# Attention hybrid of four images: turns of token blocks taken from TensorE and given to VectorE and DMA, one diagonal block handled as the others, a scratch tensor loaded in pieces

## The chip, the cores and the metric

The kernel runs on one core of one Trainium2 chip, in float32. The metric is the time of one execution on the device in microseconds (us), taken as the median of several runs. Traces come from one profiled execution.

## What is computed

The input is four images `x` of 128 channels by 64 x 64 points (4096 tokens of 128 numbers each). The reference, cut to what matters here:

```python
x = x + conv_attention(group_norm(x))       # layer 0: softmax(q k^T) v, a gate, a projection
t = to_tokens(x)                            # (4 images, 4096 tokens, 128)
def attn(u):                                # layer 1, u = layer norm of t
    q = u @ W
    return softmax(q @ q.T) @ u
t = t + attn(ln(t))
t = t + recurrence(batch_norm(ln(t) @ Wf.T))   # y_t = sigmoid(wx_t + y_{t-1} V^T) over the tokens
```

Layer 1's score matrix `q q^T` is symmetric. The kernel uses that: it computes a block of exponentials once and uses its transpose for the mirrored block.

## The kernel before

**Tiling.** Each image has 4096 tokens, cut into 8 blocks of 512 (`NB` = 8), each of 4 groups of 128 (`NQ` = 4). For each of the four images the kernel runs layer 0 (`layer0`, with `attention`, L220) and then layer 1 (`layer1`, L560). A scan over the recurrence (L971 on) ends the program.

**Layer 1.** The rows run in the order n = 6, 7, 5, 4, 3, 2, 1, 0. A row takes its blocks a = n, n-1, ..., 0, each in two steps (i = 0, 1). A step computes scores (L810, TensorE), exponentials (L816, ScalarE), and, two steps later, the product with the tokens of block a (`direct`, L681). For a < n the exponentials are also turned: VectorE transposes 32 x 32 blocks within `dd` (L651), and 16 DMAs carry the pieces to their partitions in `tt` (`send`, L661: 12 issued by SyncE, SP, and 4 by ScalarE, ACT). Four steps later TensorE multiplies the turned tile (`reversed_products`, L694), which adds to row a. There are two `dd` buffers and three `tt` buffers.

**Diagonal blocks.** For a = n > 1 (`upper`) only the upper triangle of the 4 x 4 groups is computed (score widths 512, 384, 256, 128), the six groups above the diagonal are turned in the same way, and `own_products` (L671, three products of widths 384, 256, 128) adds the lower triangle, three steps after the block. For the blocks n = 1 and n = 0, `quarter` (L585) computes the full first half and lets TensorE transpose four 128 x 128 groups (L596).

**End of a row block.** When all parts of block n are summed in `oacc` (`part`, L701), `finish` (L712) puts three functions in a queue. `tokens` (L733) lets TensorE transpose the four groups of `oacc` (L736), takes the denominators (L741), adds the residual `t` and normalises (`layernorm`, L298, with one power on GpSimd, POOL). `turn` (L755) lets TensorE transpose the four groups of the normalised tokens (L758), ScalarE copies them out of PSUM (L759), and `result` sends `t` off by `turn_out`. `inputs` (L765) multiplies by the recurrence's weights (L767) and stores the product in `wxs_d`.

**A move.** Layer 0 already turns its blocks of 128 x 512 without TensorE (`move`, L289): `turn_out` (L275) transposes 32 x 32 blocks on VectorE (L280), issues four DMAs on SP (L284) that write a DRAM scratch `turn_d` with the blocks in their turned places, and one more DMA on SP (L294) reads the scratch back to the destination.

**What sets the order.** Deferred functions wait in the deque `pending`; work of the next image (`prepare`: norms, projections, gates, put up at L941) waits in `ahead`. A step of layer 1 runs one function of `pending`, else one of `ahead` (L842); an empty function `nothing` stands as a delay and gives its turn to `ahead`. Layer 0 takes `ahead` first. `flush` (L215) runs what must be complete before a row. A scheduler then orders the instructions of each engine by its own estimates, except in a few parts written as fixed. TensorE, VectorE, ScalarE and SP each execute their instructions in that order.

**The last image.** At the start of its layer 1, three DMAs of 2 MB (L947) load the recurrence's inputs of images 0 to 2 from `wxs_d` into `wxs`, which takes the buffer of layer 0's operands.

Of the kernel before, what the change touches and what calls it, by code (L numbers as in the profile page):

```python
# [10 lines left out]
F32 = mybir.dt.float32  # L11
I32 = mybir.dt.int32
AF = mybir.ActivationFunctionType
ALU = mybir.AluOpType
# [4 lines left out]
P = 128  # L19
# [150 lines left out]
        )  # L170


def fast(
    tc, x, out, t_d, t2_d, wxs_d, turn_d, wt, col, par, par2, bpc, bc, ident, gavg, quart,
    own, shift, inv_sqrt, par_ok, load, scales, shifts, written,
# [15 lines left out]
    with ExitStack() as st:  # L191
# [10 lines left out]


        ahead: deque = deque()
        pending: deque = deque()

        def nothing():

# [6 lines left out]
        def flush(until=None):  # L215

            while pending and until not in done:
                pending.popleft()()

        def attention(score_mm, bias, scale, weigh, finish, need):  # L220


            fifo: deque = deque()
            o = None
            left = len(pending)

            def pop():
                nonlocal o
                n, p, e, acc = fifo.popleft()
                if p == 0:  # L230
                    o = None
                o = weigh(o, n, p, e)
                if p == PAIRS - 1:
                    finish(n, o, acc)

            for n in range(NB):
                acc = first = None
                for p in range(PAIRS):
                    need(n, p)
                    ps = ps_s.tile([P, 2, QB], F32, tag="s", name="ps")  # L240
                    for h in range(2):
                        lhsT, rhs = score_mm(n, p, h)
                        nc.tensor.matmul(ps[:, h, :], lhsT=lhsT, rhs=rhs, start=True, stop=True)  # L243
                    e = ep.tile([P, 2, QB], F32, tag="e", name="e")
                    nc.scalar.activation(e, ps, AF.Exp, scale=scale)  # L245
                    if p == 0:
                        first = e
                    elif p == 1:
                        acc = accp.tile([P, 2, QB], F32, tag="acc", name="acc", bufs=2)
                        nc.vector.tensor_tensor(acc, first, e, ALU.add)  # L250
                    else:
                        nc.vector.tensor_tensor(acc, acc, e, ALU.add)  # L252
                    fifo.append((n, p, e, acc))
                    if len(fifo) > LAG:
                        pop()
                        if p == 0:
                            pop()
                    if ahead:
                        ahead.popleft()()
                    elif pending and (p % 2 == 0 or left > 0 or len(pending) > 6):  # L260
                        left -= 1
                        pending.popleft()()
            while fifo:
                pop()

# [204 lines left out]
        def layer0(b, gate, q, k, v, need):  # L470
# [20 lines left out]
            def finish(n, o, acc):  # L491
# [60 lines left out]
                    nc.gpsimd.tensor_scalar(hn, hn, 1.0, None, ALU.add)  # L552
                    done.add((b, n))

                pending.extend([sums, nothing, denominators, projection, nothing, tokens])

            attention(score_mm, None, SCALE, weigh, finish, need)
            return h, qt
# [1 line left out]
        def layer1(b, h, qt):  # L560
# [6 lines left out]
            tt = big.tile([P, 3, NQ * QB], F32, tag="tt", name="tt")  # L567
            fifo: deque = deque()
            own_turned: deque = deque()

            unsent: deque = deque()
            turned: deque = deque()
# [40 lines left out]

            def upper(n, a):

                return a == n > 1

# [45 lines left out]
            def own_products():  # L665

                _, n, t, o = own_turned.popleft()
                assert fifo and fifo[-1][0] == n
                t = t[:, : 4 * 6 * 32].rearrange("q (p s k) -> q p s k", p=4, s=6)
                for j, s in ((3, 3), (2, 1), (1, 0)):  # L670
                    nc.tensor.matmul(  # L671
                        o[:, : j * P], lhsT=h[:, NQ * n + j, :],
                        rhs=t[:, :, s : s + j, :].rearrange("q p k j -> q k p j"),
                        start=False, stop=False,
                    )
# [25 lines left out]
            def part(n, o):  # L701
# [7 lines left out]
                if parts[n] == NB - n - (b == B - 1 and n == 0):  # L709
                    finish(n)  # L710

            def finish(n):  # L712
                cs = bass.ts(n, QB)
                rinv = stat.tile([P, NQ], F32, tag="rinv", name="rinv")
                t = work.tile([P, 4, NQ, 32], F32, tag="t", name="t1", bufs=2)
                if b == B - 1 and n == 0:
# [5 lines left out]
                    def bank():  # L722
                        return ps_o.tile([P, QB], F32, tag="o", name="ml")
# [9 lines left out]
                def tokens():  # L733
                    m = bank().rearrange("q (j c) -> q j c", j=NQ)
                    for j in range(NQ):
                        nc.tensor.transpose(m[:, j, :], oacc[:, n, bass.ts(j, P)], ident)  # L736
                    if b == B - 1 and n == 0:
                        take_banks()
                    at = (B + b) * NT + n * NQ
                    den = den_all[:, at : at + NQ]  # L740
                    nc.vector.tensor_reduce(den, m, AX.X, ALU.add)  # L741
                    nc.vector.tensor_scalar(den, den, 1.0 / C, None, ALU.mult)
                    nc.vector.reciprocal(rinv, den)
                    for j in range(NQ):
                        nc.vector.scalar_tensor_tensor(
                            t1[:, j, :].rearrange("q (p i) -> q p i", p=4),
                            m[:, j, :].rearrange("q (p i) -> q p i", p=4), rinv[:, j : j + 1],
                            t[:, :, j, :], ALU.mult, ALU.add,
                        )
                    layernorm(quarters(t1), quarters(h2))  # L750
# [12 lines left out]
                    result()  # L763

                def inputs():  # L765
                    m = bank()
                    nc.tensor.matmul(m, lhsT=wt["f"], rhs=th, start=True, stop=True)  # L767
                    nc.vector.bn_stats(bn_st[:, b * NB + n, :], m)
                    m = m.rearrange("p (g i s) -> p i g s", i=L // 2, s=2)
                    if b == B - 1 and n == 0:  # L770
                        last_inputs.append(m)
                    elif b == B - 1:
                        nc.vector.tensor_copy(wxs[:, :, b, bass.ts(n, GB), :], m)
                    else:
                        wx = work.tile([P, L // 2, GB, 2], F32, tag="wx", name="wx")
                        nc.vector.tensor_copy(wx, m)
                        nc.sync.dma_start(wxs_d[b, :, :, bass.ts(n, GB), :], wx)

                if b == B - 1 and n == 0:
                    pending.appendleft(tokens)  # L780
                    pending.extend([turn, inputs])
                elif b == B - 1 and n == 1:
                    pending.extend([tokens, nothing, turn, inputs])
                elif b == B - 1 and n < 4:
                    pending.extend([tokens, turn, inputs])
                else:
                    pending.extend([tokens, nothing, nothing, nothing, turn, inputs])


            for n in [NB - 2, NB - 1] + list(range(NB - 3, -1, -1)):  # L790
# [4 lines left out]
                for a in order(n):  # L795
# [4 lines left out]
                    for i in range(2):  # L800
                        ps = ps_s.tile([P, 2, QB], F32, tag="s", name="ps")
                        e = ep.tile([P, 2, QB], F32, tag="e", name="e")
                        if a == n < 2 and i == 1:
                            quarter(n, ps, e, before)
                        else:
                            width = 0
# [24 lines left out]
                            queries(NB - 1)  # L831
                        fifo.append((n, a, i, e, o))
                        clock += 1
                        if len(fifo) > LAG:
                            direct()
                            if a == order(n)[0] and i == 0:
                                direct()
                        if own_turned and own_turned[0][0] <= clock:
                            own_products()
                        if turned and turned[0][0] <= clock:  # L840
                            reversed_products()
                        if pending:  # L842
                            pending.popleft()()
                        elif ahead:
                            ahead.popleft()()
                    if turns(n, a) or upper(n, a):
                        send(n, a, d, t, nc.sync, range(3))
                        unsent.append(partial(send, n, a, d, t, nc.scalar, (3,)))
                    if upper(n, a):
                        own_turned.append((clock + 3, n, t, o))  # L850
                    elif turns(n, a):
# [5 lines left out]
            if b == B - 1:  # L857

                ordered.enter_context(tc.manual_schedule())
            pending.extend([reversed_products] * len(turned))  # L860

# [71 lines left out]
        for b in range(B):  # L935
# [3 lines left out]
            if b < B - 1:  # L939
                parts0, norm, chunks, gates = prepare(b + 1, own_bank)  # L940
                ahead.extend(norm + sum(chunks, []) + gates)  # L941
            else:


                wxs = keep.tile([P, L // 2, B, G, 2], F32, tag="next", name="wxs")
                for i in range(B - 1):
                    nc.sync.dma_start(wxs[:, :, i, :, :], wxs_d[i])  # L947
            layer1(b, h, qt)
            while ahead:
                ahead.popleft()()  # L950
# [491 lines left out]
```

## Time and profile before

| what | value |
|---|---|
| median of 3 runs | 3017.7 us (3017.13 to 3018.09) |
| profiled execution | 3015.99 us, its span 3014.3 us |
| mean granted TensorE clock | 0.995 |
| TensorE (PE) busy | 2961.1 us of the span |
| VectorE (DVE), ScalarE (ACT), GpSimd (POOL) busy | 1716.2, 1016.1, 223.1 us |
| layer 0 of image 1 (777 to 1101 us) | 324 us, PE busy 324.00 |
| layer 1 of image 1 (1101 to 1500 us) | 399 us, PE busy 396.83, DVE 200.10, ACT 111.17 |
| layer 1 of image 3 (2544 to 2932 us) | 388 us, PE busy 381.08 |

A row of the profile's timeline gives the start, the time from the first start to the last end, the engine, the line, the operation, the tiles written and read, and the count; brackets hold the engine's idle time before it and what ended it. A float32 matmul appears as two records, a transpose on TensorE as one. "SPq" and "ACTq" are the DMA issues of SP and ACT; they do not count as busy time.

### The profile page before, as it was taken

The page shows a single profiled execution, that of the slowest core. Times are in us where ns is not written, and L with a number is a line of the kernel's source. Part 1 is how long each engine was busy: PE and PEld are TensorE (multiplying, and loading weights), DVE is VectorE, ACT ScalarE, POOL GpSimd, SP SyncE. Part 2 cuts the span into 40 slices and gives each one's busy share as a digit, 9 for nine tenths or more (in the row PEclk, how much of TensorE's full clock was granted, in tenths as well). Part 3 has the DMA queues.
Part 4 walks back from the last instruction along what each step waited for, and adds up shares of the span by engine and source line. Part 5 has one row for each costly group of instructions (what it writes and reads, how often), then busy time and mean ns, then how long its engine had stood idle before and what let it go on. Part 6 is the DMA issues. An engine that isn't in the chain of part 4 may idle for free.

```text
span 3014.3 us, 32549 instructions
## 1 busy us (share of the span) xinstructions
PE 2961.1 (98%) x10774; PEld 1378.9 (46%) x10774; DVE 1716.2 (57%) x3208; ACT 1016.1 (34%) x1123; POOL 223.1 (7%) x216
## 2 busy tenths in 40 slices
PE   8999999999999999999999999999999999999995
PEld 4444444444444444444444444444444444444443
DVE  6666654544666664544466666554556666344456
ACT  4444422222344432222244443222234444222224
POOL 0111100000011110000011101000001111000000
PEclk9999999999999999999999999999999999999998
DMA  1112144434122134444312114444422113544434
GB/s 42 41 54 57 50 130 105 100 95 111 31 56 57 43 90 112 102 104 106 74 46 56 42 47 127 104 106 99 106 46 56 41 48 91 147 108 104 111 94 186
DMA packets 265425, 250.62 MB, mean 83 GB/s; under 512 B 96160, under 2 KB 180640, under 8 KB 264224
## 3 DMA queue, kind: packets, MB, share of 16 engines
q1 hardware_dynamic: 239328, 216.95, 27.2%
q10 hardware_dynamic: 25920, 31.49, 4.2%
q8 instruction: 89, 1.46, 0.2%
q14 instruction: 88, 0.72, 0.1%
HBM read 65.80 MB, written 56.62 MB: 41 GB/s over the span
## 4 chain that ended last, share of the span: by engine, by line
PE 94%; DVE 2%; DMA 1%; ACT 1%; SPq 0%; issue 0%; ACTq 0%; POOL 0%; DVEq 0%
PE o L485 29%; PE o L681 15%; PE ps L243 15%; PE ps L810 14%; PE ot L694 13%; PE o L671 1%; PE m L272 1%; PE m L767 1%; PE mp L378 1%; PE mp L447 1%; DMA wxs<-wxs_d 1%; PE mp L432 1%; DVE t2s L1020 1%; DVE ps_r L991 1%; PE mq L582 1%; PE m L736 1%
## 5 line engine op out<-in xcount | busy, mean ns | idle before, releaser
L485 PE MATMUL o<-e,nxt 64*128 64x512 f32 x4096 | 966.4, 589 | 0.0
L245 ACT ACTIVATE e<-ps 128x1024 f32<-128x1024 f32 x512 | 521.6, 1025 | 687.6 <-PE ps L243 656.1
L252 DVE TENSOR_TENSOR acc<-acc,e 128x1024 f32<-128x1024 f32 x448 | 547.3, 1222 | 231.7 <-ACT e L245 216.0
L485 PEld LDWEIGHTS o<-e,nxt 64*128 64x128 f32 x4096 | 400.1, 187 | 483.0 <-issue 474.2
L816 ACT ACTIVATE e<-ps,shift 128x1024 f32<-128x1024 f32 (+2 forms) x282 | 298.7, 1060 | 729.2 <-PE ps L810 431.2
L243 PE MATMUL ps<-nxt 64*128 64x512 f32 x2048 | 533.1, 595 | 1.2 <-ACT e L245 0.6
L681 PE MATMUL o<-e,h 128*128 128x512 f32 (+3 forms) x1160 | 511.4, 567 | 0.0
L810 PE MATMUL ps<-qt 128*128 128x512 f32 (+3 forms) x1128 | 501.9, 567 | 4.0 <-ACT qt L583 2.7
L651 DVE STREAM_TRANSPOSE dd<-e 128x512 f32<-128x512 f32 x444 | 287.3, 687 | 306.2 <-ACT e L816 217.5
L694 PE MATMUL ot<-tt,h 128*128 128x512 f32 x888 | 402.2, 593 | 0.0
L681 PEld LDWEIGHTS o<-e,h 128*128 128x128 f32 x1160 | 220.2, 191 | 259.0 <-issue 248.3
L810 PEld LDWEIGHTS ps<-qt 128*128 128x128 f32 x1128 | 208.1, 190 | 230.0 <-issue 208.1
L243 PEld LDWEIGHTS ps<-nxt 64*128 64x128 f32 x2048 | 194.9, 187 | 229.6 <-issue 148.7
L694 PEld LDWEIGHTS ot<-tt,h 128*128 128x128 f32 x888 | 164.2, 190 | 186.9 <-issue 185.5
L145 POOL TENSOR_SCALAR rstd<-mv 128x4 f32<-128x4 f32 x64 | 14.6, 228 | 2349.7 <-DVE mv L309 2349.7
L703 DVE TENSOR_TENSOR oacc<-oacc,ot 128x512 f32<-128x512 f32 x87 | 59.3, 682 | 162.2 <-PE ot L694 162.2
L541 DVE SCALAR_TENSOR_TENSOR t<-yt,rinv,t 128x128 f32<-128x128 f32 x128 | 36.5, 347 | 79.6 <-DMA yt<-turn_d 79.6
L502 POOL TENSOR_SCALAR xb<-xb,bpc 128x512 f32<-128x512 f32 x32 | 63.4, 1981 | 245.1 <-DMA xb<-in_x_dram 230.5
L552 POOL TENSOR_SCALAR h<-h 128x512 f32<-128x512 f32 x32 | 72.4, 2262 | 63.8 <-DVE d L280 63.8
L146 POOL TENSOR_TENSOR rstd<-rstd,mhalf 128x4 f32<-128x4 f32 x64 | 66.4, 1038 | 5.3
L390 ACT ACTIVATE nxt<-mp,par 64x512 f32<-64x512 f32 x31 | 23.9, 772 | 114.7 <-DVE nxt L386 101.2
L312 DVE TENSOR_SCALAR h<-t,mv,rstd 128x128 f32<-128x128 f32 x128 | 35.7, 343 | 46.9 <-POOL rstd L146 46.9
(165 smaller groups left out, 1578.4 us busy)
## 6 DMA issues: line engine op xcount, KB each, us to landing
tt<-dd SPq DMA_DIRECT2D x1332, 64.0 KB, 2.0
tt<-dd ACTq DMA_DIRECT2D x444, 64.0 KB, 2.0
turn_d<-d SPq DMA_DIRECT2D x384, 64.0 KB, 1.8
nxt<-in_x_dram SPq DMA_DIRECT2D x16, 512.0 KB, 5.5
xb<-in_x_dram SPq DMA_DIRECT2D x32, 256.0 KB, 3.3
t<-turn_d SPq DMA_DIRECT2D x32, 256.0 KB, 2.7
yt<-turn_d SPq DMA_DIRECT2D x32, 256.0 KB, 2.6
t_d<-t SPq DMA_DIRECT2D x32, 256.0 KB, 2.0
```

What stands on the lines that cost most here:

```text
L146: nc.gpsimd.tensor_tensor(dst, dst, mhalf[:, :n], ALU.pow)
L243: nc.tensor.matmul(ps[:, h, :], lhsT=lhsT, rhs=rhs, start=True, stop=True)
L245: nc.scalar.activation(e, ps, AF.Exp, scale=scale)
L252: nc.vector.tensor_tensor(acc, acc, e, ALU.add)
L485: nc.tensor.matmul(o[r], lhsT=v[rs, p + h * PAIRS, :], rhs=e[rs, h, :], start=(p == 0 and h == 0), stop=(p == PAIRS - 1 and h == 1),)
L502: biased = nc.gpsimd.tensor_scalar(xb, xb, bpc, None, ALU.add)
L552: nc.gpsimd.tensor_scalar(hn, hn, 1.0, None, ALU.add)
L651: nc.vector.transpose(d.rearrange("q f b k j -> q k b f j")[:, 2 * i + half], e[:, half, :].rearrange("q (b f j) -> q b f j", b=NQ, f=NQ),)
L681: nc.tensor.matmul(o[:, cols], lhsT=h[:, NQ * a + 2 * i + half, :], rhs=es, start=(a == order(n)[0] and i == 0 and half == 0), stop=(a == ...
L694: nc.tensor.matmul(ot, lhsT=h[:, NQ * n + j, :], rhs=t.rearrange("q (p b k j) -> q b k p j", p=4, b=NQ, k=NQ)[:, j], start=(j == 0), stop= ...
L810: nc.tensor.matmul(scores, lhsT=qt[:, bass.ts(at, P)], rhs=qt[:, n * QB + cols.start : n * QB + cols.stop], start=True, stop=True,)
L816: nc.scalar.activation(e.rearrange("p a b -> p (a b)")[:, :width], ps.rearrange("p a b -> p (a b)")[:, :width], AF.Exp, bias=shift,)
```

## The change

Seven edits:

1. `finish_moved` replaces `finish` for all eight blocks of images 0 to 2 and for blocks 4 to 7 of image 3. Both transposes on TensorE become moves: `oacc` is moved in `sums`, the normalised tokens in `tokens`. The copy out of PSUM by ACT is gone. Blocks 0 to 3 of image 3 keep the old way.
2. `pending` becomes a `Work` object: chains of (delay, function) in which a later chain may run beside an earlier one as long as it stays two functions behind. Its clock advances by 2 in a step of layer 1 and by 1 in a step of layer 0.
3. The diagonal block n = 1 is now `upper`; `quarter` serves n = 0 alone.
4. `own_products` stands ahead of the step's `direct` products.
5. Of a turned tile with a < n, SP issues 8 DMAs and ACT 8. Diagonal tiles keep 12 and 4.
6. The load of `wxs` is cut into 12 DMAs of 0.5 MB, taken one at a time through `ahead`.
7. In layer 0, the deferred functions get the delays 0, 4, 2, 4.

```diff
+    def may(self, c):
+        b = c["before"]
+        if c["ready"] > self.now:
+            return False
+        if b is None or not b["tasks"]:
+            return True
+        return c["behind"] is not None and b["count"] > c["count"] + c["behind"]
...
-                pending.extend([sums, nothing, denominators, projection, nothing, tokens])
+                pending.add([(0, sums), (4, denominators), (2, projection), (4, tokens)], behind=None)
...
             def upper(n, a):
-                return a == n > 1
+                return a == n > 0
...
+            def finish_moved(n):
+                cs = bass.ts(n, QB)
+                rinv = stat.tile([P, NQ], F32, tag="rinv", name="rinv")
+                t = ot = th = None
+                def sums():
+                    nonlocal t, ot
+                    t = work.tile([P, 4, NQ, 32], F32, tag="t", name="t1", bufs=2)
+                    nc.sync.dma_start(t, t_d[b, n])
+                    ot = work.tile([P, 4, NQ, 32], F32, tag="og", name="otk")
+                    move(oacc[:, n, :].rearrange("c (j f k) -> c j f k", j=NQ, f=4), flat(ot))
+                def tokens():
+                    nonlocal th
+                    reciprocals(n, ot.rearrange("q p j i -> q j p i"), AX.XY, rinv)
+                    for j in range(NQ):
+                        nc.vector.scalar_tensor_tensor(
+                            t[:, :, j, :], ot[:, :, j, :], rinv[:, j : j + 1], t[:, :, j, :],
+                            ALU.mult, ALU.add,
+                        )
+                    h2 = work.tile([P, 4, NQ, 32], F32, tag="h2", name="h2m")
+                    layernorm(tiles(t), tiles(h2))
+                    th = work.tile([P, QB], F32, tag="th", name="thm")
+                    move(h2.rearrange("q p j i -> q j p i"), th)
+                    turn_out(t.rearrange("q p j i -> q j p i"), t2_d[b, :, cs])
+                def inputs():
+                    recurrence_inputs(n, th, ps_m.tile([P, QB], F32, tag="m", name="mw"))
+                pending.add([(0, sums), (8, tokens), (8, inputs)])
...
             def finish(n):
+                if b < B - 1 or n >= 4:
+                    return finish_moved(n)
...
                 elif b == B - 1 and n < 4:
-                    pending.extend([tokens, turn, inputs])
+                    pending.add([(0, tokens), (2, turn), (2, inputs)])
...
-                        if a == n < 2 and i == 1:
+                        if a == n == 0 and i == 1:
                             quarter(n, ps, e, before)
...
+                        if own_turned and own_turned[0][0] <= clock:
+                            own_products()
                         if len(fifo) > LAG:
                             direct()
                             if a == order(n)[0] and i == 0:
                                 direct()
-                        if own_turned and own_turned[0][0] <= clock:
-                            own_products()
...
-                        if pending:
-                            pending.popleft()()
-                        elif ahead:
-                            ahead.popleft()()
+                        if not pending.run():
+                            nothing()
+                        pending.now += 2
                     if turns(n, a) or upper(n, a):
-                        send(n, a, d, t, nc.sync, range(3))
-                        unsent.append(partial(send, n, a, d, t, nc.scalar, (3,)))
+                        own = 3 if upper(n, a) else 2
+                        send(n, a, d, t, nc.sync, range(own))
+                        for f in range(own, NQ):
+                            unsent.append(partial(send, n, a, d, t, nc.scalar, (f,)))
...
-                for i in range(B - 1):
-                    nc.sync.dma_start(wxs[:, :, i, :, :], wxs_d[i])
+                pieces = [
+                    (wxs[:, bass.ts(r, L // 8), i, :, :], wxs_d[i, :, bass.ts(r, L // 8)])
+                    for i in range(B - 1) for r in range(4)
+                ]
+                ahead.extend(partial(nc.sync.dma_start, *piece) for piece in pieces)
```

`reciprocals` and `recurrence_inputs` hold the former lines 739 to 743 and 767 to 777 unchanged.

## The prediction

> **What bounds the kernel now.** I read the page's first and fourth parts, then the waits of PE, the timeline around the edited lines, and the chain in order of time.
>
> ```profile
> PE 2961.1 (98%) x10774; PEld 1378.9 (46%) x10774; DVE 1716.2 (57%) x3208; ACT 1016.1 (34%) x1123; POOL 223.1 (7%) x216
> ...
> PE 94%; DVE 2%; DMA 1%; ACT 1%; SPq 0%; issue 0%; ACTq 0%; POOL 0%; DVEq 0%
> ```
>
> PE is busy for 98% of the span and carries 94% of the chain. So a matmul taken off PE is worth its issue time, and a matmul that waits costs its wait. What PE waits for in layer 1 is one line:
>
> ```profile
> PE o L671 <- DMA tt<-dd: 3.8, 2, 2.7
> ```
>
> Those are the first diagonal blocks (n = 6) of images 1 and 3. The timeline shows how tight they are, and what an issue costs:
>
> ```profile
> 1427.75 0.60 PE L736 MATMUL m<-ident,oacc 128*128 128x128 f32 x4
> ...
> 1428.11 2.53 ACTq L661 DMA_DIRECT2D tt<-dd  x4
> ...
> 1428.19 2.74 PE L694 MATMUL ot<-tt,h 128*128 128x512 f32 x6
> ...
> 1437.99 1.00 SPq L284 DMA_DIRECT2D t_d<-d  x2
> ...
> 1443.22 1.46 PE L671 MATMUL o<-tt,h 128*128 128x384 f32 x6
> ...
> 1444.52 0.60 PE L758 MATMUL m<-ident,h 128*128 128x128 f32 x4
> ```
>
> Four transposes occupy PE for 1428.19 - 1427.75 = 0.44 us. A send costs ACT 2.53/4 = 0.63 us of issue, a write of a move costs SP 0.50 us.
>
> ```profile
> 2551.70 9.08 DMA wxs<-wxs_d
> 2560.80 13.84 DMA wxs<-wxs_d
> ```
>
> ```profile
> 2580.47 2.05 PE L671 MATMUL o<-tt,h 128*128 128x384 f32 x3 [2.65 <-DMA tt<-dd]
> ```
>
> ```profile
> 2580.00:2610.00 30.00, 29.53 (x65) 13.74 (x66) 12.14 (x30) 5.57 (x5) 2.76 (x3) 0.89 0.50 128
> ```
>
> In image 3 the three loads of `wxs` sit ahead of the diagonal's sends and PE waits 2.65 us. The last row, a window of busy times, has the granted clock as the third number from its end: 0.89. The clock records put a half-rate stretch of 6.8 us there.
>
> **The change, part by part.**
>
> *Turns off PE.* 28 blocks lose 8 transposes each. The start-to-start times of all 248 such records of the 31 ordinary blocks sum to 29.4 us, 0.95 us a block (the rows above give 0.88). 28 x 0.95 = **-26.6 us**. All of it is on the path.
>
> [...] a move is a VectorE transpose of 0.69 us, four issues (2.0), a landing (1.8, the page's median), a read-back (2.7), some 7.2 us against 0.44 us. If those 7.2 us, twice a block, stood on the path, the sum would be 28 x 14.4 = 403 us worse. They don't if someone else is next to run: the delays of 8 units are four steps of about 5 us, so each move has about 20 us. I follow the row of PE.
>
> *Diagonal block n = 1.* A 512-wide matmul is two records of 0.43 us. Before: scores 2 x 0.86 + 2 x 0.43, four transposes 0.44, products 4 x 0.86, sum 6.5 us. After: scores, products and own products of widths 1280, 1280 and 768, sum 3328/512 x 0.86 = 5.6 us. Saved 0.85 x 4 images = **-3.4 us**.
>
> *Loads of wxs in pieces.* In the built order three pieces (1.5 MB) stay ahead of the first diagonal, where the loads of the next image (2 MB) stand in images 0 to 2, with waits of at most 1.2 us. So the wait goes, and the half-rate stretch (6.8 x 0.5 = 3.4 us of work). The excess of PE's starts over the nominal 0.43 us in that stretch is 5.6 us: **-5.6 us**, bounds -6.0 and -3.5 (if 1.2 us of wait and 0.9 us of the next item remain). The other nine pieces go between sends; four tiles there had 2.6 to 5.2 us between landing and use.
>
> *Own products earlier.* In the built order of the first diagonal of each image they stand one matmul (0.86 us) earlier. In images 0 to 2 the data landed just in time (0.2 us ahead of the start), so PE waits 0.86 us more: **+2.6 us**.
>
> *The other diagonals.* Between the last landing and the own products there were 7.1, 8.2, 6.1 and 3.6 us for n = 5, 4, 3, 2 in image 0, and 1.2, 1.4, 0.8 and 2.0 us in image 3. The own products now come 1.72 us earlier (two direct products), PE loses 0.44 us ahead of them, and the order of the built instructions puts four writes and a read-back (2.35 us) on SP ahead of the diagonal's sends: 4.5 us less. Where SP was late from the tile before, it gains 4 x 0.62 = 2.5 us. That leaves 2.6, 3.7, 1.6 and 1.6 us in image 0, about the same for n = 1, and -0.8 to 1.5 us in image 3. The price is between 0 and about 2 us at each of 18 diagonals (36 us). I take **+2 us**, near the lower end, because the sums above are mostly positive.
>
> *Queues.* SP issues 396 fewer sends (-245 us), 224 more writes (+112) and 56 read-backs (+19, at 0.34 us each): it is relieved, by over 100 us in all. Hidden either way behind PE, as long as the writes, which wait for VectorE's layer norm, don't hold the sends behind them. ACT issues 460 more: per tile of 10.3 us of PE (12 matmuls) it has 8 x 0.63 + 2 x 1.11 = 7.2 us. That fits, hidden by PE. A late exponential costs PE only when it is later than one step, about 5 us. VectorE gets two transposes more per block, less the copy's place in PSUM: 28 x 1.4 = 39 us, in stages where it is busy half the time (200 of 399 us). Copies of 0.59 us fall off ACT, also off the path. The chains' order in layer 0 moves work among engines that wait for PE: zero, and if a chain were late it would be the row's `flush`, which has 14 steps.
>
> *End of image 3.* Blocks 3 and 2 keep their transposes, but the built order leaves 5.6 us of PE work between the first and the second group, and VectorE's chain between them takes 6.4 us when undisturbed (reduce to first normalised group 5.7, plus 0.6). That is a wait of 0.8 us or more, before there was none; with the turns of tiles in between, 1.5 us each: **+3 us** (bounds 0 and 8).
>
> **The sum.** -26.6 - 3.4 - 5.6 + 2.6 + 2 + 3 = -28.0 us. Against the profiled execution (3015.99 us; its span is 3014.3) that gives 2988.0; the median of the runs is 1.7 us higher, so 3017.7 - 28.0 = 2989.7 us.
>
> [...] Here an idle stretch of 2.65 us was enough, and one of 1.2 us (image 1) was not. [...] By the row those near 2 us may cost 3.4 us more each. I take none, and put three of them (10 us) into the range.
>
> **The rivals.**
>
> *A. The diagonals and the tail eat half.* For: image 3 had under 2.3 us of slack at each diagonal, more DMA traffic slows landings, and ACT's eight issues can delay an exponential. Against: SP is relieved. With 0.8 us at each of 18 diagonals (14) and the tail at 5: -26.6 - 3.4 - 5.6 + 2.6 + 14 + 5 = -14, so 3004 us.
>
> *B. Slower: SP becomes the bound at the diagonals.* The mechanism: SP holds the sends behind a move's writes, which wait for VectorE. If the landings at the 18 moved diagonals come 4 us later than reckoned, with 1.5 us of slack each waits 2.5 us (45 us), and at about that wait the clock halves, say at four of them (14 us). With the reckoned 2 us of diagonals replaced: -28 - 2 + 59 = +29, so 3047 us. It decides from about 3.2 us of extra lateness on, where 18 x 1.7 = 30 us cancel the gain. For it: VectorE's chain of 6.5 us stands ahead of the writes. Against: the built order puts the second move between tiles with 9 to 12 us of slack in images 0 to 2, and ahead of the diagonal only the first move, which waits for a single add.
>
> *C. More gain.* If all new waits (2.6 + 2 + 3) are absorbed and the waits at the layers' start shrink too: -36 to -38, so 2981 us.
>
> That the transposes stay on PE is excluded: the built order has 24 of the 248 left.
>
> **How the numbers follow.** Forecast (2983 to 2997 by its own bounds) 0.65; A (2997 to 3012) 0.19; B 0.07; C (below 2983) 0.06; the rest, within 0.2% (6 us, about what a measurement of this kernel can tell from no change), 0.03. Within A nearly all is faster. So faster 0.89, same 0.04, slower 0.07. The range reaches down to 2979 (into C) and up to 3007 (most of A); that leaves out B, the end of A and a little of C, under 0.2.
>
> **What would show it right or wrong.** The rows of PE's transposes fall to 12 of each kind; PE busy falls by about 30 us. PE's wait at the own products: near 2 us at the first diagonals, under 1 us elsewhere. If it names `tt<-dd` in tens of us, B or A holds. The window at the start of image 3's layer 1 has a clock of 1.00. Layer 1 of image 1 falls from 399 to about 391 us. Wrong would be: waits of PE on ACT's exponentials, which I take as zero.

## The result, and the profile after it

The changed kernel takes 3000.62 us (median of 4 runs, 2997.57 to 3003.48), the kernel before 3017.89 us on the same chip. The ratio is 0.9943, with a 95% interval of 0.9925 to 0.996. The gain is 17.3 us where 28.0 us were forecast. The time is inside the predicted range (2979 to 3007 us), 10.9 us above the predicted one. The profiled execution took 2999.84 us, its span is 2998.1 us.

Line numbers below are those of the changed kernel. Its lines in short: layer 0 has scores in L290, exponentials in L292, VectorE's sums of the exponentials in L299 and products in L532. A move is transposed in L327, written in L331 and read back in L341. The denominators of a moved block are reduced in L795, and L800 is its product with the recurrence's weights. In layer 1, L897 is the scores, L719 the own products, L709 the sends. The transposes that stay on PE are L838 (`oacc`) and L856 (tokens).

The page's first and fourth parts, after:

```profile
PE 2933.5 (98%) x10558; PEld 1358.1 (45%) x10558; DVE 1760.0 (59%) x3280; ACT 995.1 (33%) x1091; POOL 219.4 (7%) x216
...
PE 89%; DVE 5%; DMA 2%; ACT 1%; SPq 1%; issue 1%; POOL 0%; ACTq 0%; DVEq 0%
```

PE is busy for 27.6 us less, as forecast (about 30), and yet the span is only 16.2 us shorter. The fourth part says where to look: PE's share of the chain fell from 94 to 89%, VectorE's rose from 2 to 5%, and DMA's from 1 to 2%. At some places the chain now leaves PE and goes through VectorE and a DMA. The waits of PE name the place:

```profile
PE ps L290 <- ACT e L292: 9.9, 5, 3.6
...
PE o L719 <- DMA tt<-dd: 3.1, 4, 1.1
...
PE m L856 <- DVE h L359: 2.8, 3, 1.1
```

The columns are us in all, times, and the longest. The first line had this form before the change:

```profile
PE ps L243 <- ACT e L245: 0.6, 1, 0.6
```

This wait is not in layer 1, which the change is about, but in layer 0, whose lines were hardly edited. The time from each stage's first PE instruction to the next stage's shows the same:

| stage | before, us | after, us | difference |
|---|---|---|---|
| layer 1, images 0 to 3 | 375.2, 375.5, 374.4, 370.8 | 368.6, 369.1, 368.8, 364.5 | -24.9 |
| layer 0, image 0 | 365.95 | 365.94 | 0 |
| layer 0, images 1 to 3 | 346.9 each | 348.7, 349.4, 351.6 | +9.1 |
| end and scan | 94.0 | 93.6 | -0.4 |

Blocks 1 and 0 of an image end its layer 1, so their deferred work runs in the next image's layer 0. Six of the 28 moved blocks are of that kind: the sum of the prediction has 22 x 0.95 and all other terms (-22.3 us) in layer 1, and 6 x 0.95 = -5.7 us in layer 0. Layer 1 gave 2.6 us more than its share. Layer 0 missed by 14.8 us, which is more than the whole miss.

The 2.6 us are a shift across the boundary. Of the product with the recurrence's weights, the trace of before has 12 records in each layer 1 of images 0 to 2 and 4 in each layer 0 behind it; after, it has 10 and 6. So one product per image (two records, 0.86 us; 3 x 0.86 = 2.6) moved from layer 1 to layer 0. The share of layer 0 holds all the same, because its transposes cost more than was reckoned: two runs below put four of them at 0.79 us there and a product at 1.26 us (neighbours included), and (16/4) x 0.79 - 1.26 = 1.9 us an image is the 5.7 us of the sum.

The timeline of the changed kernel at the start of image 1's layer 0 (rows of ACT, DVE, PE and SP; brackets hold the idle time before the row and what ended it):

```profile
773.04 0.71 DVE L327 STREAM_TRANSPOSE d<-oacc 128x512 f32<-128x512 f32 x1 [0.54 <-DMA turn_d<-d]
...
774.27 1.80 SPq L331 DMA_DIRECT2D t_d<-d  x1
...
776.11 1.91 SPq L331 DMA_DIRECT2D turn_d<-d  x4
...
779.46 0.34 SPq L341 DMA_DIRECT2D otk<-turn_d  x1
...
782.15 0.69 DVE L795 TENSOR_REDUCE den_all<-otk 128x4 f32<-128x512 f32 x1 [5.95 <-DMA otk<-turn_d]
...
783.82 1.22 DVE L299 TENSOR_TENSOR acc<-acc,e 128x1024 f32<-128x1024 f32 x1
...
785.13 1.02 ACT L292 ACTIVATE e<-ps 128x1024 f32<-128x1024 f32 x1 [3.23 <-DVE acc L299]
...
791.82 1.02 ACT L292 ACTIVATE e<-ps 128x1024 f32<-128x1024 f32 x1 [5.67 <-DVE acc L299]
...
792.89 1.13 PE L290 MATMUL ps<-nxt 64*128 64x512 f32 x4 [2.63 <-ACT e L292]
```

Block 0's first move leaves VectorE at 773.75. SP is not free for its four writes before 776.11, since the last write of another turn holds it for 1.80 us first, and the read-back goes out at 779.46. It lands at about 782.1. VectorE's queue has the reduction that wants this data (L795) next, and stands for 5.95 us. The sums of layer 0's exponentials (L299) are queued behind it. They come late (VectorE runs nothing from 776.20 to 782.15, and the exponentials that ScalarE had written by 776.75 are summed from 783.82 on), the buffers of exponentials do not come free, ScalarE waits 3.23 and then 5.67 us for VectorE, and TensorE waits 2.63 us for ScalarE. The second wait is the longer one because block 0's layer norm and its two further transposes also stand ahead of the next sum (L299 at 783.82, then at 790.54). Before the change the same work stood in this queue without the wait, as the row of the reduction shows:

```profile
786.21 0.69 DVE L741 TENSOR_REDUCE den_all<-m 128x4 f32<-128x512 f32 x1
```

The same happens in image 2 (the reduction stood for 5.96 us, TensorE for 2.46) and image 3 (7.03 and 3.60 us). VectorE's waits sum it up:

```profile
DVE den_all L795 <- DMA otk<-turn_d: 34.8, 17, 7.0
```

From start to start, PE loses 2.8, 0.75, 2.6 and 3.76 us at these places in layer 0 (over the 0.43 us of an undisturbed step from one matmul to the next; the idle times by the matmuls' modelled ends are 2.63, 0.59, 2.46 and 3.60). After two of them the clock record shows half rate, for 3.41 and 6.83 us. By the matmuls' start times that cost 1.8 and 3.0 us, near half of each. The sum is 9.9 + 4.8 = 14.7 us, the size of the miss. Two windows of the changed kernel show the clock as the third number from the end:

```profile
1510.00:1517.00 7.00, 6.41 (x18) 2.38 (x20) 5.62 (x6) 2.58 (x3) 0.00 (x0) 0.76 0.58 137
2220.00:2236.00 16.00, 12.40 (x43) 4.73 (x40) 12.62 (x27) 4.09 (x4) 1.37 (x3) 0.79 0.30 75
```

The stretch of image 3 in which the loads of `wxs` had stood is clean now. The timeline and the window that answer to those of before:

```profile
2557.39 1.54 PE L719 MATMUL o<-tt,h 128*128 128x384 f32 x6 [1.15 <-DMA tt<-dd]
```

```profile
2557.00:2587.00 30.00, 29.61 (x72) 13.63 (x73) 12.98 (x31) 7.21 (x8) 2.76 (x3) 1.00 0.69 185
```

The wait is 1.15 us instead of 2.65, and the clock is 1.00 instead of 0.89.

### The profile page after: what moved, and what is told of

The parts are those of the page before. It is cut to its first block, busy times and chain, and to the rows that moved or that the text cites. A ratio compares the mean times of both kernels' runs of the same rounds, so it can differ in the third digit from the quotient of the medians.

```text
span 2998.1 us, 32623 instructions
## 1 busy us (share of the span) xinstructions
PE 2933.5 (98%) x10558; PEld 1358.1 (45%) x10558; DVE 1760.0 (59%) x3280; ACT 995.1 (33%) x1091; POOL 219.4 (7%) x216
## 4 chain that ended last, share of the span: by engine, by line
PE 89%; DVE 5%; DMA 2%; ACT 1%; SPq 1%; issue 1%; POOL 0%; ACTq 0%; DVEq 0%
PE o L532 27%; PE o L729 15%; PE ps L897 14%; PE ps L290 14%; PE ot L742 12%; PE o L719 1%; DMA tt<-dd 1%; PE m L319 1%; PE mp L425 1%; PE mp L494 1%; DVE acc L299 1%; PE mp L479 1%; PE mw L800 1%; PE mq L630 1%; SPq L709 1%
## 5 line engine op out<-in xcount | busy, mean ns | idle before, releaser
L532 PE MATMUL o<-e,nxt 64*128 64x512 f32 x4096 | 969.5, 591 | 0.0
L292 ACT ACTIVATE e<-ps 128x1024 f32<-128x1024 f32 x512 | 520.3, 1023 | 702.8 <-PE ps L290 628.9
L299 DVE TENSOR_TENSOR acc<-acc,e 128x1024 f32<-128x1024 f32 x448 | 549.5, 1227 | 209.0 <-ACT e L292 191.0
L532 PEld LDWEIGHTS o<-e,nxt 64*128 64x128 f32 x4096 | 401.0, 187 | 484.4 <-issue 475.6
L290 PE MATMUL ps<-nxt 64*128 64x512 f32 x2048 | 533.2, 596 | 10.4 <-ACT e L292 9.9
L897 PE MATMUL ps<-qt 128*128 128x512 f32 (+3 forms) x1144 | 504.8, 563 | 4.9 <-ACT qt L631 2.7
L729 PE MATMUL o<-e,h 128*128 128x512 f32 (+3 forms) x1160 | 505.2, 561 | 0.0
L897 PEld LDWEIGHTS ps<-qt 128*128 128x128 f32 x1144 | 213.6, 190 | 248.1 <-issue 218.3
L290 PEld LDWEIGHTS ps<-nxt 64*128 64x128 f32 x2048 | 195.4, 187 | 245.1 <-issue 153.3
L693 DVE STREAM_TRANSPOSE dd<-e 128x128 f32<-128x128 f32 (+1 forms) x112 | 35.2, 352 | 55.1 <-ACT e L903 48.9
```

The source lines that it names most:

```text
L532: nc.tensor.matmul(o[r], lhsT=v[rs, p + h * PAIRS, :], rhs=e[rs, h, :], start=(p == 0 and h == 0), stop=(p == PAIRS - 1 and h == 1),)
L729: nc.tensor.matmul(o[:, cols], lhsT=h[:, NQ * a + 2 * i + half, :], rhs=es, start=(a == order(n)[0] and i == 0 and half == 0), stop=(a == ...
L897: nc.tensor.matmul(scores, lhsT=qt[:, bass.ts(at, P)], rhs=qt[:, n * QB + cols.start : n * QB + cols.stop], start=True, stop=True,)
```

## The experiments

My theory after this comparison (theory 1) is that block 0's moves cost what is missing, because VectorE stands at a reduction that waits for a read-back, with the sums queued behind it. The rival (theory 2) is that not this instruction but the moves as such are at fault, being too slow for the short steps of layer 0. Further runs test the terms of the sum one by one. In all of these kernels the whole function is computed. Each ratio is to the kernel before, run on the same chip; that kernel's median moved by up to 1.7 us between the series (3016.18 to 3017.89).

### Block 0, or blocks 0 and 1, left to TensorE

```diff
-                if b < B - 1 or n >= 4:
+                if 1 < n and (b < B - 1 or n >= 4):
                     return finish_moved(n)
```

> Blocks 0 and 1 of images 0 to 2, whose last parts fall into the next image's layer 0, turn on TensorE as before; the other 22 blocks are moved. Theory 1: the 14.7 us go, 6 x 0.95 = 5.7 us of transposes come back, so 2989 to 2994 us. Rival (layer 0's waits come from its own chains and their new delays): 3000 + 5.7 = 3004 to 3008 us.

Measured: 2993.55 us, ratio 0.9926 (0.9912 to 0.9939). Layer 0 of images 1 to 3 takes 347.3 us each, PE's wait for exponentials there is 0.6 us as before the change, and the mean granted clock is 0.996 (0.995 in the changed kernel). Six blocks put back on TensorE make the kernel 7 us faster than the changed one (6 us when each is set against its own series).

With `0 < n` in place of `1 < n`, only block 0 goes back:

> Block 0 alone of images 0 to 2 turns on TensorE, 25 blocks are moved. If the wait of layer 0 comes from block 0's read-back (the traces show it there, none at block 1's): the 14.7 us go and 3 x 0.95 = 2.85 us come back, so 2989 to 2992 us, below the run with two blocks on TensorE (2993.6). Rival (block 1's move holds up layer 0 as well): 2994 to 3000 us.

Measured: 2991.62 us, ratio 0.9921 (0.9908 to 0.9935); layer 0 takes 346.55 us three times. VectorE's waits at the reduction, in this kernel:

```profile
DVE den_all L795 <- DMA otk<-turn_d: 14.1, 16, 1.7
```

The longest wait fell from 7.0 to 1.7 us, and TensorE's wait went with it. So the 14.7 us belong to three moved blocks of the 28. Block 1's second move lies in layer 0 too and costs no wait there, so theory 2 does not hold for moves in general. The difference of layer 0 between the two runs, 347.34 - 346.55 = 0.79 us an image, is what four transposes of block 1 cost (12 against 8 in this stage; the other four lie in layer 1). By the same count, layer 0 before the change had four transposes more than the run with two blocks on TensorE and one product of the recurrence less: 347.34 - 346.87 + 0.79 = 1.26 us for a product.

### The reduction put in its place in the program's order

```diff
-                nc.vector.tensor_reduce(den, o, axes, ALU.add)
+                reduced = nc.vector.tensor_reduce(den, o, axes, ALU.add)
+                if axes == AX.XY:
+                    tc.keep_in_program_order(reduced)
```

> The denominators' reduce of a moved block keeps its program place on VectorE; nothing else changes. Theory 1 (VectorE stands at the head of its queue waiting for the read-back of block 0's first move, in the first steps of layer 0, the adds behind it hold the exponentials' buffers, and TensorE waits): the 14.7 us that layer 0 of images 1 to 3 lost go, time 2984 to 2990 us, TensorE's wait at the scores of layer 0 on the exponentials falls from 9.9 us to under 1. Rival (VectorE has simply too much work there with two more transposes a block): the same work stays, so 2997 to 3003 us, the wait only moves.

Measured: 3013.78 us, ratio 0.999 (0.9983 to 0.9996). The expectation failed by over 20 us. VectorE no longer waits for `otk` at all and TensorE hardly for exponentials (1.8 us), as theory 1 wanted. But PE's first wait is now another:

```profile
PE mw L802 <- DMA thm<-turn_d: 11.0, 3, 3.7
```

The product with the recurrence's weights (here L802) wants the second move. It stands in TensorE's queue, and TensorE waits for the read-back itself, three times. The mean granted clock is 0.994, against 0.996 in the run with block 0 on TensorE. Layer 0 takes 359.2, 357.3 and 358.5 us. About 4.7 us of each are the time of layer 1 products that this order puts behind layer 0's first scores (14 records), so that layer 1 being 3.4 to 4.3 us shorter here is no gain. The wait was not removed; it was handed to the engine that bounds the kernel.

### Both users of a move in the program's order

As above, and the product too:

```diff
-                nc.tensor.matmul(m, lhsT=wt["f"], rhs=th, start=True, stop=True)
+                wanted = nc.tensor.matmul(m, lhsT=wt["f"], rhs=th, start=True, stop=True)
+                if b < B - 1 or n >= 4:
+                    tc.keep_in_program_order(wanted)
```

> As the run that kept the reduce in its program place, and the product that takes a moved block's result on TensorE keeps its place too. There the wait had passed from VectorE to TensorE, which stood before that product for its read-back (3.7 us three times, each with a half-rate stretch). If the trouble is only that in-order queues are filled by estimates that put a move's landing too early: with both kept, layer 0 falls to about 347 us an image and the time to 2984 to 2990 us. Rival (a move is too slow for layer 0's steps wherever its users stand): 2995 us or more.

Measured: 3010.32 us, ratio 0.9979 (0.9972 to 0.9985). Theory 1's number was missed; the time lies in the range of theory 2. But the product's place can also just be too early:

```profile
PE mw L802 <- DMA thm<-turn_d: 11.2, 3, 3.8
```

### The same, with a longer delay

```diff
-                pending.add([(0, sums), (8, tokens), (8, inputs)])
+                pending.add([(0, sums), (8, tokens), (10, inputs)])
```

> As the run with both users of a move in program order (3010.3 us), with the delay ahead of the recurrence's product 10 instead of 8: two steps of layer 0 more, about 5 us. The waits of TensorE for thm were 11.2 us in all, 3.8 the longest, each with a half-rate stretch. If the place in program order was only too early, 5 us take these waits away and layer 0 falls from 358 to about 350 us: 2988 to 2995 us. If a move is late because VectorE's work behind it is late, wherever its user stands, the waits stay: 3005 us or more.

Measured: 3027.66 us, ratio 1.0043 (1.0029 to 1.0056), slower than before the change. Neither expectation held. The waits for `thm` did go, so the place of the product was too early, as theory 1 said. But layer 0 takes 361.4, 364.9 and 363.9 us, in sum longer than in any other kernel of the study. The timeline of PE shows it:

```profile
804.43 1.13 PE L290 MATMUL ps<-nxt 64*128 64x512 f32 x4
805.39 1.45 PE L532 MATMUL o<-e,nxt 64*128 64x512 f32 x3
806.25 0.69 PE L290 MATMUL ps<-nxt 64*128 64x512 f32 x1
806.68 0.59 PE L532 MATMUL o<-e,nxt 64*128 64x512 f32 x1
806.79 1.34 PE L290 MATMUL ps<-nxt 64*128 64x512 f32 x3
807.96 1.88 PE L532 MATMUL o<-e,nxt 64*128 64x512 f32 x4
810.95 2.41 PE L532 MATMUL o<-e,nxt 64*128 64x512 f32 x5 [1.11 <-ACT og L541]
```

Layer 0's products use 64 of the 128 rows (64*128 in the timeline). An undisturbed row has eight of them in 1.88 us; here four take as long. One of them takes 0.59 us, so one starts every (1.88 - 0.59)/3 = 0.43 us, where the undisturbed row starts two in that time. Windows of 10 us count 35, 38 and 36 matmul records at such places (from 800, 810 and 860 us), against 50 and 49 from 790 and 900 us, all at a granted clock of 1.00. The longer delay thus changed the scheduler's order at the row ends of layer 0. Why it chose this order I did not find out, so these three runs do not tell what a correctly placed user of block 0's moves would cost.

### The own products after the step's first direct product

```diff
-                        if own_turned and own_turned[0][0] <= clock:
-                            own_products()
                         if len(fifo) > LAG:
                             direct()
+                            if a == order(n)[0] and i == 0 and not (own_turned and own_turned[0][0] <= clock):
+                                direct()
+                        if own_turned and own_turned[0][0] <= clock:
+                            own_products()
                             if a == order(n)[0] and i == 0:
                                 direct()
```

> The own products stand behind the step's first direct product again (ahead of it in the changed kernel). If they arrive too early for their data (waits and clock-neutral stalls of about 7 us in the changed trace: 0.5 to 1.1 us at each first diagonal, 0.8 to 1.4 at n = 1, 1.1 at n = 7 of image 3), 0.86 us or more at each of some 8 sites comes back: 2993 to 2998 us, all in layer 1. Rival (the data are late by what the earlier place does not set, or the later place delays the row's end): 2999 to 3003 us.

Measured: 2989.51 us, ratio 0.9907 (0.9894 to 0.9921), 11 us faster than the changed kernel and better than expected. Layer 1 falls by 1.4 to 1.8 us per image, in all 6.4 us. Layer 0 falls too: PE's wait for exponentials is 7.3 us in all and 2.1 at the longest (9.9 and 3.6 in the changed kernel), and the mean granted clock is 0.996 (0.995). VectorE's wait at the reduction is 32.5 us in all, nearly as before this edit (34.8). So the reductions still wait, but TensorE feels less of it.

### The diagonal block n = 1 by quarter, as before the change

```diff
             def upper(n, a):
-                return a == n > 0
+                return a == n > 1
...
-                        if a == n == 0 and i == 1:
+                        if a == n < 2 and i == 1:
                             quarter(n, ps, e, before)
```

> The diagonal block n = 1 by the old way again (half of it computed in full, four transposes on TensorE). By work alone it costs 3.4 us: 3004 us. But the trace shows about 3.0 us of new waits at this block in images 0 to 2 (0.8, 1.4, 0.8), which go with it: 2999 to 3002 us is expected.

Measured: 2996.28 us, ratio 0.9932 (0.9917 to 0.9947). The edit was forecast to cost 3.4 us by work alone, and the median is 4 us lower. The runs of the two kernels overlap (2994.01 to 2999.21 against 2997.57 to 3003.48), so they speak against a cost of 3.4 us, but do not show a gain. Layer 1 is the same within 0.8 us per image: in the changed kernel, three waits around n = 1 (0.78, 1.41 and 0.80 us in images 0 to 2) take up what the narrower matmuls save. Two thirds of them (0.57, 0.85 and 0.59 us) are not at the own products but at the four transposes of n = 0 just ahead of them, where TensorE waits for ScalarE. The line of the changed kernel for it, which the kernel before does not have:

```profile
PE ps L644 <- ACT e L903: 1.5, 3, 0.7
```

And layer 0 is 1.2 to 2.5 us faster per image, with PE's wait for exponentials at 6.2 us in all and 2.1 at the longest (9.9 and 3.6 in the changed kernel). Twelve sends fewer stand on SP just ahead of the moves of blocks 1 and 0; that this is why is argued, not shown.

### The loads of wxs whole

```diff
-                pieces = [
-                    (wxs[:, bass.ts(r, L // 8), i, :, :], wxs_d[i, :, bass.ts(r, L // 8)])
-                    for i in range(B - 1) for r in range(4)
-                ]
-                ahead.extend(partial(nc.sync.dma_start, *piece) for piece in pieces)
+                for i in range(B - 1):
+                    nc.sync.dma_start(wxs[:, :, i, :, :], wxs_d[i])
```

> The scratch of the recurrence's inputs is loaded in three pieces of 2 MB again, ahead of the first diagonal of image 3. If the pieces saved the wait and the half-rate stretch (4.3 us by the two traces): 3003 to 3006 us, all of it in image 3's layer 1. Rival (the pieces between the sends cost as much as they saved): 2998 to 3001 us.

Measured: 3011.85 us, ratio 0.9982 (0.9975 to 0.9989). The pieces are worth 11 us here, where 3 to 6 were expected. PE's wait at image 3's first diagonal, in this kernel:

```profile
2574.34 2.90 PE L719 MATMUL o<-tt,h 128*128 128x384 f32 x6 [10.38 <-DMA tt<-dd]
```

It was 2.65 us in the kernel before, where the loads were whole too. Half rate lasts 13.65 us instead of 6.83: the clock is 0.77 from 2560 to 2590 us here, where the kernel before has 0.89 from 2580 to 2610. The trace divides the 7.7 us between the two waits. Counted from the issue of the first load, the diagonal's last send landed after 33.2 us instead of 28.5, since SP issued one of its 12 sends before the third load landed instead of five. And TensorE reached the own products after 23.0 us instead of 26.1; 0.86 us of this is their earlier place.

### SP with 12 of the 16 sends, as before

```diff
-                        own = 3 if upper(n, a) else 2
+                        own = 3
```

> The sends of turned tiles are split 12 on SP and 4 on ScalarE again, all else as changed. If SP's relief is what keeps the moves out of TensorE's way: SP has 2.5 us more per tile of 10.3 us, the moved diagonals lose 2.5 us or more of slack of 0.3 to 4 us, so waits of 1 to 3 us at 18 sites, 20 to 50 us: 3020 to 3050 us. Rival (SP has room anyway): 2999 to 3004 us.

Measured: 3058.29 us, ratio 1.0137 (1.0122 to 1.0153), slower than before the change.

```profile
PE o L719 <- DMA tt<-dd: 40.9, 13, 8.0
```

That is rival B's line, `tt<-dd` in tens of us, and the mean granted clock is 0.989 (0.995 in the changed kernel). The mechanism of rival B is real. It is edit 5, by which ACT takes over four of the sends, that keeps the changed kernel from it.

### The two edits that gained, together

Block 0 on TensorE (`0 < n`) and the own products after the first direct product.

> Both one-part edits that gained: block 0 of images 0 to 2 keeps its transposes on TensorE (alone 2991.6 us), and the own products stand after the step's first direct product (alone 2989.5 us). If the two act at different places (layer 0's start; layer 1's diagonals), the gains add: layer 0 of images 1 to 3 near 346.6 us each, layer 1 near 367.2 us each, some 2991.6 - 6 = 2985 to 2988 us. If the later own products help because layer 0's moves land in time, the gains overlap and the time stays at 2989 to 2992 us.

Measured: 2985.08 us (2984.25 to 2987.82), ratio 0.9899 (0.9884 to 0.9914). This is the best version of the study, faster than both kernels. Layer 0 takes 346.55 us three times, layer 1 takes 367.5, 367.1, 368.3 and 362.3 us. So layer 0 is as in the run with block 0 on TensorE, and layer 1 is within 1.4 us an image of the run with the own products later. The two gains taken alone (9.0 and 11.1 us on the changed kernel) make 15.5 us together, not 20.1, because the later own products by themselves also relieved layer 0. The page's fourth part and PE's waits of this kernel:

```profile
PE 94%; DVE 3%; ACT 1%; DMA 1%; SPq 0%; ACTq 0%; issue 0%; POOL 0%; DVEq 0%
```

```profile
PE ps L897 <- ACT e L903: 1.4, 4, 0.4
PE o L719 <- issue: 1.4, 3, 0.9
...
PE ps L290 <- ACT e L292: 0.6, 1, 0.6
```

PE has its 94% of the chain back, and the wait for exponentials is the 0.6 us it was before the change.

Two variants of it:

> Blocks 0 and 1 of images 0 to 2 on TensorE (alone 2993.6 us) with the own products after the first direct product. Block 1's eight transposes cost 3 x 0.95 = 2.9 us against block 0 alone on TensorE; if block 1's moves cost nothing in layer 0, this is 2 to 3 us above the version with block 0 alone: 2987 to 2991 us. If block 1's moves still cost something there, it is equal to it.

Measured: 2990.29 us, ratio 0.9919 (0.9906 to 0.9933). With block 1 on TensorE as well, it is 5.2 us slower: 3 x 0.8 us lie in layer 0, and TensorE waits 2.5 us in layer 1 for VectorE's last sum ahead of block 1's transposes. The move of block 1 pays.

> As the version with block 0 on TensorE and the own products later, and the diagonal block n = 1 by quarter as before. The prediction gave n = 1 a gain of 3.4 us; in the changed kernel, quarter cost nothing in layer 1 because n = 1's waits ate the gain. With the own products later these waits should be smaller, so here quarter should cost up to 3 us: 2986 to 2991 us. If it costs nothing or gains, the triangle at n = 1 is worth nothing in any version.

Measured: 2990.48 us, ratio 0.9915 (0.9901 to 0.9928), 5.4 us slower. So the triangle at n = 1 seems to pay once the own products do not come early, but this is not shown: of the 6.7 us between the two traces 4.2 lie in image 1's layer 1, where a wait of 1.6 us of another kind (for a copy of ScalarE) came up, and layer 1 of images 0 and 2 differs by +0.3 and -0.5 us.

## Why the prediction was right and wrong

The direction and the main mechanism were right: matmuls taken off an engine that is busy 98% of the time are worth their issue time. Point by point:

- **Turns off PE, and n = 1.** PE busy fell by 27.6 us. Layer 1 as a whole is 24.9 us shorter. With its other terms as measured (below: -4.3, +0.75, +4.1, +1.7), some 27 us are left for the 22 blocks and n = 1, where 24.3 were forecast. Of the 3 us between, 2.6 are the three products that went over to layer 0.
- **n = 1, by itself: -3.4 us.** Wrong in the changed kernel, where waits around it ate it; where the own products come later, the one run is in favour of it but does not settle it.
- **Loads of wxs: -5.6 us.** The excess time of that stretch fell from 5.64 to 1.31 us, -4.3 us, within the bounds. The run with whole loads shows that the term was defined against the wrong alternative: in the changed kernel, whole loads would have cost 11 us.
- **Own products earlier, first diagonals: +2.6 us.** Measured +0.75. **Other diagonals: +2 us.** Measured about +4.1, of which n = 1 alone has 3.0. Together 4.9 for 4.6. That the sums agree is luck: 2.0 of the 3.0 us at n = 1 are waits for exponentials, which the prediction had at zero, and not waits for sends. Putting the own products later gained 6.4 us in layer 1, so edit 4 costs a little more than this.
- **End of image 3: +3 us.** PE's waits for VectorE's layer norm went from 1.1 to 2.8 us, +1.7.
- **The failed step is under "Queues":** "The chains' order in layer 0 moves work among engines that wait for PE: zero". It priced the chains by what they do and by the latest time at which they must be done (`flush`, 14 steps). It did not ask what is queued behind a deferred instruction while it waits for a DMA. The prediction itself had worked out 7.2 us for a move and said that "someone else is next to run"; on VectorE, which stood for 5.95 us ahead of the sums, no one was. And "a late exponential costs PE only when it is later than one step, about 5 us" used layer 1's step. A step of layer 0 takes 2.57 us, and ScalarE stood for up to 5.67 us before an exponential. The term that was put at zero measured 14.7 us.
- **The clock.** The prediction took no half-rate cost for its waits. Waits of 2.46 us (image 2) and 3.60 us (image 3) were followed by half rate, one of 2.63 us (image 1) was not. The row of before, a wait of 2.65 us with 6.83 us of half rate, spoke for such a cost, and the range was right to hold three such stretches; two came. But it is luck in part that the time fell within the range: its upper end was put there for the clock and for rival A, not for the place where the time was lost.
- **The rivals.** A named the right size (3004 us) with the wrong place. It counted on slower landings under more traffic: in the kernel before, the median from a send's issue to its landing was 2.8 us from 2544 to 2600 us, at 185 GB/s, and 2.0 us from 610 to 770, at 97 GB/s; for whole tiles over the span it went from 2.0 us before to 2.1 us after. B did not come, for the reason given (SP is relieved), and the run with 12 sends shows it.
- What the prediction named as a sign that it would be wrong, "waits of PE on ACT's exponentials, which I take as zero", is what the profile shows.

## What to carry to other kernels

When work moves from the bounding engine to a round trip of DMAs, ask at each user of the data which engine's queue it stands in and what is queued behind it. The move is nearly free where the next instructions on that engine are of no hurry, and can pass much of the remaining flight on where they feed the bounding engine within a step or two: here VectorE's stands of 5.95, 5.96 and 7.03 us cost TensorE 3.6, 4.4 and 6.8 us, half rate included. The moves of 25 of the 28 blocks brought no such wait, and those of three cost over half of what all 28 were reckoned to gain (14.7 of 26.6 us), so leave out the few at the change to a stage with shorter steps before trying to order them better.

## What was not expected of the hardware

The length of a wait alone does not tell whether half rate follows. In the changed kernel it followed waits of TensorE of 2.46 us (image 2) and 3.60 us (image 3), for 3.41 and 6.83 us, and stayed out after one of 2.63 us (image 1; the clock is 1.00 from 782.5 to 795.5 us). In the kernel before it followed one of 2.65 us, for 6.83 us.

| kernel, wait of TensorE | the wait, us | half rate, us |
|---|---|---|
| before, image 3, 2.65 us | 2577.82 to 2580.47 | 2579.62 to 2586.44 |
| changed, image 1, 2.63 us | 790.26 to 792.89 | none |
| changed, image 2, 2.46 us | 1508.13 to 1510.59 | 1511.95 to 1515.36 |
| changed, image 3, 3.60 us | 2226.39 to 2229.99 | 2228.75 to 2235.57 |

Half rate began 1.80 us into the wait in the first row, 2.36 us into it in the last, and 1.36 us after its end in image 2. What sets the wait of 2.63 us apart from the others was not shown. A forecast can thus give a wait of about 2.5 us only a chance of a cost on top; it was 1.8 us in image 2 and 3.0 us in image 3.
